# An FFN for two batches as seven block products, with weight sums kept as int8 and widened by GpSimd

## The chip, the cores and the metric

The kernel runs on one core of one Trainium2 chip. The metric is the device time of one execution in microseconds (us); the median of three runs is given. A core has TensorE (PE, matrix products; its weight loads are listed as PEld), VectorE (DVE), ScalarE (ACT), GpSimd (POOL) and SyncE (SP, which here only issues DMAs). Each engine works through its own instructions in order and waits for the others by semaphores. SBUF is the on-chip memory that all of them read, PSUM the one that PE writes its sums to.

## The reference

A cross-attention layer and a feed-forward layer (FFN), 16 batches of 128 rows, width 1024, float32:

```python
x = x + xattn(layernorm(x), ctx, ctx, Wq, bq, Wk, bk, Wv, bv, Wo, bo)   # 32 query heads, 8 key heads of 32
x = x + ffn(layernorm(x), kernel, scale)

def ffn(x, kernel, scale):                 # kernel: 1024 x 1024 booleans, one in ten is true
    x_ei = concat([x[..., :819], -4.0 * x[..., 819:]], axis=-1)
    return scale * einsum('bsi,if->bsf', x_ei, kernel.astype(float32))
```

So the FFN's weights are 0, 1 or, in the last 205 rows, -4 and 0 once the factor is moved into them. Their block sums and differences are small integers.

## The kernel before

Batches go in eight groups of two (`GB = 2`). For a group the kernel projects keys, values and queries, does attention in four units (a batch and half of the heads each), projects the output (`out_proj`) and does the FFN. Stages of three groups run at the same time: while the attention of group g runs, PE is given the output projection of group g-1, the key, value and query projections of group g+1, and then the FFN of a finished group.

The order of all engines' instructions is written out by hand. `Stream` holds a queue of generators and a list of timed events. A generator (`prep_v`, `ffn`, ...) issues a few matmuls and yields the microseconds that the author gives them; `Stream.run` takes pieces from the queue, adds these to `stream.now`, and fires every event that is due (`later(us, fn)`). `attend` starts an attention unit and sets the events for its maxima, exponentials, division and transposes. What stands in an event or a generator is thus issued at a planned time; at run time each engine keeps that order and waits for what isn't there.

- Query and output projections are done by `seven`: a 2x2 block product in seven products instead of eight (Winograd's form, L462). Left or right sums `s1..s4`, `t1..t4` come from DVE (L507, L644) or, for weights, from DRAM where they were stored once (`combine`, L782). Two PSUM buffers (`ps_mm`, `bufs=2`) hold the running sums `u` and `c`, then `v`; after each product `read` lets DVE add the buffer into the result (L676 for the output projection), and PE may go on in that buffer only when DVE has read it.
- The FFN (`ffn`, L738) is done batch by batch: two column halves x 8 chunks of 128 rows x 2 parts = 32 matmuls of 128x128 by 128x512 at L323. The activations are split in two float32r parts, `x2h` (rounded, ACT, L729) and `x2l` (the rest, DVE, L732), whose products add to the full accuracy; the weights, exact in float32r, lie in SBUF as `wf_sb`, converted once from bytes by ACT (`convert_ffn`, L258). DVE scales and adds each half into the residual `x` (L751), and SP writes it out (L759).
- Normalizing a row (`normalize`, L285) takes DVE for statistics, one small POOL operation for the root (`rs_a` for the input, `rs_f` for the FFN, L291) and DVE again (L292). The normalized rows of all but the last group go through DRAM and come back as 32x32 blocks in a `turn` tile (`through_dram`, L302), which DVE transposes. The last group's are transposed by PE (`ffn_transpose`).
- `get_x` (L887) loads the input rows of a later group (`xn`, in a `turn` tile too) and sets `rows_x`, statistics and normalization, 5 and 9 us behind. `load_residual` (L172) loads `x` a second time, for the residual, into one of three `x` tiles, and POOL adds the output bias (L180) in four pieces.

In the loop over groups the order at the end of a group is `qs[nxt]`, `get_x`, `prep_ctx`, then the FFN of both batches; the FFN of the last three groups comes in the last group's attention and behind it.

Of the kernel before, what the change touches and what calls it, by code (L numbers as in the profile page):

```python
# [10 lines left out]
FR = mybir.dt.float32r  # L11
U8 = mybir.dt.uint8
AF = mybir.ActivationFunctionType
ALU = mybir.AluOpType
# [8 lines left out]
class Stream:  # L23
# [28 lines left out]
    def run(self, until, keep=lambda: False):  # L52

        while self.now < until or keep():
            while self.events and min(self.events)[0] <= self.now:
                self.fire()
            if not self.piece():
                if not self.events:
                    return
                self.fire()  # L60

    def drain(self):
        while self.queue or self.events:
            self.run(self.now + 1.0)


def mixed(dense, light, skip=0, every=1):


    for n, us in enumerate(dense):  # L70
        yield us
        if n >= skip and (n - skip) % every == 0:
            yield next(light, 0.0)
    yield from light

# [7 lines left out]
def kernel(  # L83
# [47 lines left out]
    wv_sb = const.tile([P, NC, KV], FP, name="wv_sb")  # L131
    wf_sb = const.tile([P, NC, F], FR, name="wf_sb")
    bqT = const.tile([P, NA, NG], FP, name="bqT")
# [4 lines left out]

    xs, xns, cs = {}, {}, {}


# [24 lines left out]
    def load_x(b, tag="row"):  # L166

        x_t = work.tile([P, D], FP, tag=tag, name=f"xn{b}", bufs=2)
        nc.sync.dma_start(out=x_t, in_=x[b])
        xns[b] = x_t  # L170

    def load_residual(b, us=4.0, tag="x"):  # L172
# [37 lines left out]


    PIECE = 1024
    RING = 8
# [44 lines left out]
    def convert_ffn():  # L258

        row_w = const.tile([P, 1], FP, name="row_w")  # L260
        nc.gpsimd.memset(row_w, 1.0)
        nc.gpsimd.affine_select(
            out=row_w,
            in_=row_w,
            compare_op=ALU.is_ge,
            fill=w_inh,
            base=n_exc % P - 1,
            pattern=[[0, 1]],
            channel_multiplier=-1,
        )  # L270
        def chunk_(c):
            raw = raws[c // (NC // 2)][:, c % (NC // 2)]
            if (c + 1) * P <= n_exc:
                nc.scalar.copy(wf_sb[:, c], raw)
            else:
                w = w_inh if c * P >= n_exc else row_w
                nc.scalar.activation(wf_sb[:, c], raw, AF.Copy, scale=w)

        for c in range(NC):
            stream.later(2.0 * c, lambda c=c: chunk_(c))  # L280

# [20 lines left out]
    def through_dram(row, name, store, back, turn, then):  # L302

        there = dram.tile([P, D], FP, name=f"dram_{name}")

        def load():
            c_t = work.tile([P, NB, NC, 32], FP, tag="turn", name=f"turn_{name}", bufs=2)
            src = there.rearrange("(t r) (k n) -> k r t n", r=32, k=NB)
            for k in range(NB):
                dst = c_t[k * 32 : (k + 1) * 32].rearrange("r t c f -> r t (c f)")  # L310
                nc.sync.dma_start(out=dst, in_=src[k])
            stream.later(turn - back, lambda: then(c_t))

        stream.later(store, lambda: nc.sync.dma_start(out=there, in_=row) and None)
        stream.later(back, load)

# [10 lines left out]
    cTs, xTs, kTs, vs, qTs = {}, {}, {}, {}, {}  # L327
    HC = NC // 2

    def turned(store, srcs, grp, h, name, batches=range(GB)):  # L330
# [3 lines left out]
        for j in batches:  # L334
            b = grp * GB + j
            src = srcs.pop(b) if h == 1 else srcs[b]
            tp = ps_tp.tile([P, HC, P], FP, tag="tp", name=f"tp_{name}{b}_{h}")
            for c in range(HC):
                at = (h * HC + c) * P
                nc.tensor.transpose(tp[:, c], src[:, at : at + P], ident)  # L340
            nc.scalar.copy(store[grp, h][:, :, j * S : (j + 1) * S], tp)
            yield 0.45

# [12 lines left out]
    def rows_x(b):  # L356
# [5 lines left out]
        row = work.tile([P, D], FP, tag="row", name=f"xq{b}", bufs=2)  # L362
        normalize(by_quadrant(row), by_chunk(src), stats, f"a{b}")
        through_dram(row, f"x{b}", 2.5, 7.0, 7.0, lambda c_t: rows.update({b: c_t}))

    def turn_x(b, h):
        grp, j = b // GB, b % GB
        if (grp, h) not in xTs:
# [4 lines left out]
            c_t[:, :, h * HC : (h + 1) * HC],  # L373
        )

    def prep_ctx(grp, *us):
# [85 lines left out]
    def seven(name, product_of, read):  # L462
# [18 lines left out]
        read(u, "c21")  # L481

    PRODUCTS = ["a11 b11", "a12 b21", "s2 t2", "s1 t1", "s3 t3", "s4 b22", "a22 t4"]

# [135 lines left out]

    x2Ts, x2ns, x2stats = {}, {}, {}

    def out_proj(grp):
# [12 lines left out]
        def run():  # L636
# [36 lines left out]
            def read(mm, c):  # L673
# [7 lines left out]
                if c in ("c12", "c21"):  # L681
                    def norm():
                        b = b0 + j
                        x2n = work.tile([P, D], FP, tag="row", name=f"x2n{b}", bufs=2)
                        if b < B - GB:
                            normalize(by_quadrant(x2n), by_chunk(x_t), stats[j], f"f{b}")
                            through_dram(x2n, f"f{b}", 3.0, *FBACK[j], lambda t: split_blocks(b, t))
                        else:
# [10 lines left out]

    def new_parts(b):  # L700
        hi = work.tile([P, NC, S], FR, tag="x2h", name=f"x2h{b}", bufs=2)
        lo = work.tile([P, NC, S], FR, tag="x2l", name=f"x2l{b}", bufs=2)
        x2Ts[b] = (lo, hi)

    def ffn_transpose(b):

        new_parts(b)
        lo, hi = x2Ts[b]
        src = x2ns.pop(b)
        for h in range(NC // 4):  # L710
            tp = ps_tp.tile([P, 4, P], FP, tag="tp", name=f"tp_f{b}_{h}")
            for j in range(4):
                c = 4 * h + j
                nc.tensor.transpose(tp[:, j], src[:, c * P : (c + 1) * P], ident)
            cut = slice(4 * h, 4 * h + 4)
            nc.scalar.copy(hi[:, cut], tp)
            nc.vector.tensor_tensor(lo[:, cut], tp, hi[:, cut], ALU.subtract)
            yield 0.45

    def split_blocks(b, c_t, h=0):  # L720

        if h == 0:
            new_parts(b)
        lo, hi = (
            part[:, HC * h : HC * (h + 1)].rearrange("p c (t n) -> p t c n", t=NB) for part in x2Ts[b]
        )
        blocks = c_t[:, :, HC * h : HC * (h + 1)]
        nc.vector.transpose(blocks, blocks)
        nc.scalar.copy(hi, blocks)  # L729

        def rest():
            nc.vector.tensor_tensor(lo, blocks, hi, ALU.subtract)  # L732
            if h == 0:
                split_blocks(b, c_t, 1)

        stream.later(2.0, rest)

    def ffn(b):  # L738
        parts, x_t = x2Ts.pop(b), xs.pop(b)
        for h in range(F // HALF):  # L740
            cut = slice(h * HALF, (h + 1) * HALF)
            mm = ps_mm.tile([P, HALF], FP, tag="mm", name=f"f_{b}_{h}")
            pairs = [(part[:, c], wf_sb[:, c, cut]) for c in range(NC) for part in parts]
            for us in accumulate(mm, pairs):
                yield us / 4

            parts_ = 2 if b == B - 1 and h == F // HALF - 1 else 1
            for k in range(parts_):
                n = HALF // parts_
                at, some = slice(h * HALF + k * n, h * HALF + (k + 1) * n), slice(k * n, (k + 1) * n)  # L750
                nc.vector.scalar_tensor_tensor(  # L751
                    x_t[:, at], mm[:, some], fscale, x_t[:, at], ALU.mult, ALU.add
                )
                if b == B - 1:
                    queue = nc.scalar if k else nc.sync
                    queue.dma_start(out=out[b][:, at], in_=x_t[:, at])
            yield 0.43
        if b < B - 1:
            nc.sync.dma_start(out=out[b], in_=x_t)  # L759

    def attend(b, a, length):
# [18 lines left out]
        return pts  # L780

    def combine(w, k, part, engine=nc.gpsimd):  # L782

# [9 lines left out]
        for dst, left, right, op in ops:  # L793
            for h in range(2):
                cols = slice(h * HALF, (h + 1) * HALF)
                engine.tensor_tensor(dst[:, cols], left[:, cols], right[:, cols], op)  # L796
            yield
        for n, t in enumerate(order):
            nc.sync.dma_start(out=sums[w, n + 1, k], in_=t)

# [15 lines left out]
    def load_o_part(k):  # L816

        part = {}
        for r in range(2):
            for o in range(2):  # L820
                tag = ("x2h", "x2l")[o]
                t = work.tile([P, PIECE], FP, tag=tag, name=f"wo{k}_{r}_{o}", bufs=2)
                nc.sync.dma_start(out=t.rearrange("p (c n) -> p c n", c=2), in_=o_block(r, o, k))
                part[r, o] = t
        return part
# [4 lines left out]
    with tc.manual_schedule():  # L830
# [67 lines left out]
        def get_ctx(grp):  # L898
            if grp < NGRP:
                for j in range(GB):  # L900
                    load_ctx(grp * GB + j)

        def residuals(grp):
            for j in range(GB):
# [22 lines left out]
        for grp in range(NGRP):  # L927
# [18 lines left out]
            elif more:  # L946
# [8 lines left out]
                    qs[nxt],  # L955
                    once(get_x, nxt + 1),
                    once(prep_ctx, nxt + 1, 2.5, 7.0, 11.0, 16.0),
                )

                if nxt < NGRP - 1:  # L960
                    stream.add(ffn(p0), once(load_residual, b1, 2.0), ffn(p1))
            else:
# [3 lines left out]
                    once(load_residual, b0, 4.0, "ctx"),  # L966
                    ffn(p0 - 2),
                    once(load_residual, b1, 4.0),
                    ffn(p1 - 2),
                )  # L970
# [21 lines left out]
            os[NGRP - 1],  # L992
            ffn(B - 4),
            mixed(ffn(B - 3), ffn_transpose(B - 2), 10, 2),
            mixed(ffn(B - 2), ffn_transpose(B - 1), 8, 2),
            ffn(B - 1),
        )
# [50 lines left out]
```

## Time and profile before

The runs took 788.64, 786.96 and 786.23 us. The profiled execution has a span of 783.8 us.

| What | us |
|---|---|
| median of the runs | 786.96 |
| span of the profiled execution | 783.8 |
| PE busy in 700.0 to 724.0 (the last group's attention, with an FFN) | 23.4 of 24.0 |
| PE busy in 748.7 to 783.8 (the last two groups' FFN, output) | 31.2 of 35.1 |
| DVE busy in these two | 15.1 and 12.6 |
| POOL busy in these two | 5.4 and 0.8 |
| FFN matmuls, L323 `f` | 512 |
| POOL operations in the whole span | 142, 114.6 us |

A line of the group view reads: source line, engine, operation, what is written from what, shape, count, then busy time and mean duration, then the engine's idle time just before these and what ended it. A chain line reads: start, duration, engine, tile and line, count. Matmul durations in the profile overlap each other, since PE is pipelined; the spacing of a run of equal matmuls tells what one costs.

### The profile page before, as it was taken

What the parts mean: (1) busy time and instruction counts of PE and PEld (TensorE: products, weight loads), DVE (VectorE), ACT (ScalarE), POOL (GpSimd) and SP (SyncE); (2) the same over time, 40 slices, a digit from 0 to 9 for tenths busy, and PEclk for the clock granted to TensorE, in tenths of its full rate; (3) what the DMA queues carried; (4) which work ended last, traced back from release to release, by engine and by line L of the source; (5) the groups of instructions that cost most, each with busy time, mean ns of one, the idle gap of its engine ahead of it and who ended that gap; (6) DMA issues with size and microseconds to landing.
All of it is one profiled execution on the core that took longest, in us unless ns stands there. A gap on an engine that the chain in (4) does not pass through costs nothing.

```text
span 783.8 us, 13740 instructions
## 1 busy us (share of the span) xinstructions
PE 765.3 (98%) x5008; PEld 570.7 (73%) x5008; DVE 488.7 (62%) x887; ACT 323.1 (41%) x1261; POOL 114.6 (15%) x142
## 2 busy tenths in 40 slices
PE   5999999999999999999999999999999999999997
PEld 4877884689747986479855898558985689456476
DVE  1358648756766667466784667755676666765552
ACT  0244854435234453344433444344434445575100
POOL 4066502010100102020020200202001010103000
PEclk9999999999999999999999999999999999999999
DMA  9999899969698777878688795977769667763702
GB/s 241 317 332 316 327 342 372 271 196 304 236 299 237 235 237 233 293 215 262 222 270 264 192 290 207 307 230 206 265 216 313 207 199 235 253 202 103 264 27 81
DMA packets 99412, 192.42 MB, mean 245 GB/s; under 512 B 8256, under 2 KB 57728, under 8 KB 99344
## 3 DMA queue, kind: packets, MB, share of 16 engines
q1 hardware_dynamic: 97568, 189.30, 75.4%
q10 hardware_dynamic: 1248, 1.11, 0.6%
q0 software_dynamic: 528, 1.12, 0.6%
q8 instruction: 40, 0.66, 0.4%
q14 instruction: 28, 0.23, 0.1%
HBM read 161.09 MB, written 30.41 MB: 244 GB/s over the span
## 4 chain that ended last, share of the span: by engine, by line
PE 87%; DMA 6%; DVE 4%; POOL 1%; issue 1%; SPq 0%; ACT 0%; DVEq 0%; POOLq 0%
PE f L323 14%; PE o_u L662 13%; PE q_u L451 13%; PE o_v L662 7%; PE tpp L601 7%; PE q_v L451 7%; PE v L323 6%; PE k L323 5%; PE sc L568 4%; PE av L611 4%; PE q_c L451 3%; PE o_c L662 3%; DMA ctx<-in_ctx_dram 2%; DMA wo<-in_L_xattn_Wo_dram 1%; DMA piece<-in_L_xattn_Wq_dram 1%; POOL wo L796 1%
## 5 line engine op out<-in xcount | busy, mean ns | idle before, releaser
L584 ACT ACTIVATE p<-sc,negm 128x128 f32<-128x128 f32 x512 | 181.4, 369 | 133.2 <-DVE negm L580 73.1
L603 ACT COPY pt<-tpp 128x512 f32<-128x512 f32 x128 | 74.7, 591 | 146.8 <-PE tpp L601 146.5
L580 DVE TENSOR_REDUCE negm<-sc 128x4 f32<-128x512 f32 x128 | 86.8, 680 | 45.6 <-PE sc L568 45.6
L584 ACT ACTIVATION_READ_ACCUMULATOR p<-sc,negm 128x1 f32 x512 | 105.5, 206 | 0.0
L323 PE MATMUL f<-wf_sb,x2l 128*128 128x512 f32 x256 | 104.3, 407 | 0.0
L323 PE MATMUL f<-wf_sb,x2h 128*128 128x512 f32 x256 | 100.5, 393 | 0.0
L596 DVE TENSOR_TENSOR p<-p,inv 128x512 f32<-128x512 f32 x128 | 91.9, 718 | 4.4
L451 PE MATMUL q_u<-t,piece 128*128 128x128 f32 x672 | 81.3, 275 | 0.0
L601 PEld LDWEIGHTS tpp<-ident,p 128*128 128x128 f32 x512 | 61.9, 141 | 24.6 <-issue 16.7
L601 PE MATMUL tpp<-ident,p 128*128 128x128 f32 x512 | 75.9, 273 | 3.4 <-DVE p L596 3.2
L451 PEld LDWEIGHTS q_u<-t,piece 128*128 128x128 f32 x672 | 78.1, 192 | 0.1
L180 POOL TENSOR_TENSOR x<-x,bo_b 128x256 f32<-128x256 f32 x64 | 54.3, 874 | 154.7 <-DMA x<-in_x_dram 154.7
L323 PE MATMUL v<-wv_sb,cT 128*128 128x256 f32 x256 | 61.2, 388 | 9.5 <-DMA wv_sb<-in_L_xattn_Wv_dram 7.7
L662 PE MATMUL o_v<-piece,s 128*128 128x512 f32 x128 | 60.3, 598 | 0.5 <-DVE x L676 0.5
L662 PE MATMUL o_u<-piece,s 128*128 128x512 f32 x128 | 59.2, 594 | 0.6 <-DVE x L676 0.6
L323 PEld LDWEIGHTS v<-wv_sb,cT 128*128 128x128 f32 x256 | 47.8, 194 | 16.2 <-DVE cT L349 9.2
L662 PE MATMUL o_u<-piece,yT 128*128 128x512 f32 x128 | 58.6, 600 | 0.0
L323 PE MATMUL k<-cT,wk_sb 128*128 128x256 f32 x256 | 58.0, 380 | 0.0
L323 PEld LDWEIGHTS f<-wf_sb,x2l 128*128 128x128 f32 x256 | 48.2, 188 | 10.5 <-issue 1.1
L323 PEld LDWEIGHTS f<-wf_sb,x2h 128*128 128x128 f32 x256 | 48.2, 188 | 9.6 <-issue 0.5
L323 PEld LDWEIGHTS k<-cT,wk_sb 128*128 128x128 f32 x256 | 47.9, 190 | 8.8 <-issue 2.6
L568 PEld LDWEIGHTS sc<-kT,qT 32*128 32x128 f32 x1024 | 31.4, 186 | 25.7 <-issue 25.7
(86 smaller groups left out, 938.1 us busy)
## 6 DMA issues: line engine op xcount, KB each, us to landing
piece<-o SPq DMA_DIRECT2D x64, 512.0 KB, 4.6
piece<-q SPq DMA_DIRECT2D x56, 512.0 KB, 5.1
piece<-in_L_xattn_Wq_dram SPq DMA_DIRECT2D x50, 512.0 KB, 5.0
piece<-in_L_xattn_Wo_dram SPq DMA_DIRECT2D x48, 512.0 KB, 4.7
xn<-in_x_dram SPq DMA_DIRECT2D x16, 512.0 KB, 6.8
x<-in_x_dram SPq DMA_DIRECT2D x16, 512.0 KB, 5.1
ctx<-in_ctx_dram SPq DMA_DIRECT2D x60, 128.0 KB, 6.7
out_dram<-x SPq DMA_DIRECT2D x15, 512.0 KB, 2.7
```

The costliest lines, as they stand in the source:

```text
L180: lambda cut=cut: nc.gpsimd.tensor_add(x_t[:, cut], x_t[:, cut], bo_b[:, cut]) and None,
L323: nc.tensor.matmul(mm, lhsT=lhsT, rhs=rhs, start=k == 0, stop=k == n - 1)
L451: nc.tensor.matmul(mm if part is None else mm[:, part], lhsT=lhsT, rhs=rhs, start=start and n == k == 0, stop=k == len(some) - 1, skip_gro ...
L568: nc.tensor.matmul(tiles[i][:, g], lhsT=qT[rows, g], rhs=kT[rows, a, cols], start=True, stop=True,)
L580: nc.vector.tensor_reduce(negm, tile_, AX.X, ALU.max, negate=True)
L584: nc.scalar.activation(p[:, g], tile_[:, g], AF.Exp, bias=negm[:, g : g + 1], accum_out=total[:, g : g + 1],)
L596: nc.vector.tensor_mul(p, p, inv.unsqueeze(2).to_broadcast([P, NG, S]))
L601: nc.tensor.transpose(tp[:, g], p[:, g], ident)
L603: nc.scalar.copy(pt, tp)
L611: nc.tensor.matmul(mm[i * HD : (i + 1) * HD], lhsT=vs[b][:, h * HD : (h + 1) * HD], rhs=pts[i], start=True, stop=True,)
L662: nc.tensor.matmul(mm, lhsT=lhsT[:, 2 * k + c], rhs=w[:, c], start=start and k == c == 0, stop=k == c == 1, skip_group_check=True,)
L796: engine.tensor_tensor(dst[:, cols], left[:, cols], right[:, cols], op)
```

## The change

The FFN takes two batches at once, as a 2x2 block product (batch by half of the inputs, half of the inputs by half of the outputs) in seven products. A product has 4 chunks x 2 parts, so a group takes 56 matmuls where two batches took 64.

The weights' blocks and sums (`b11 b21 b22 t1 t2 t3 t4`) are made once, by ACT and DVE, and lie in SBUF as int8 (seven blocks of four chunks, 14 KiB a partition where 32 were used). `widen` copies the next chunk to a float32r tile on POOL; there are eight such tiles (`WIDE`), and each chunk that PE has used calls for the next. The activations' sums `s1..s4` are made by POOL, in the `turn` tiles themselves for all but the last group, and each of the seven left blocks is split in its two parts when it is due (`split`, at most four in being). So `turn` tiles are held until the last block is split; `turning` counts their users, and `when` holds back a load until one is free. For that reason `get_x` is moved behind the FFN. The pieces of `Wo` that are summed at the start are loaded and stored as halves, in the tiles of the two parts.

```diff
+    wf_sb = const.tile([P, 7, NC // 2, F // 2], I8, name="wf_sb")
...
+    FFN = {"b11": 0, "b21": 1, "b22": 2, "t1": 3, "t2": 4, "t3": 5, "t4": 6}
+    WIDE = 8
+    wide = []
+    WANTED = [(prod.split()[1], c) for prod in PRODUCTS for c in range(NC // 2)] * (B // GB)
+    def widen():
+        if WANTED:
+            name, c = WANTED.pop(0)
+            t = work.tile([P, HALF], FR, tag="wide", name=f"wide{len(WANTED)}", bufs=WIDE)
+            nc.gpsimd.tensor_copy(t, wf_sb[:, FFN[name], c])
+            wide.append(t)
...
-        stream.later(back, load)
+        stream.later(back, lambda: stream.when(lambda: len(turning) < 2, load))
...
+    def split_now(grp, name):
+        hi = work.tile([P, HC, S], FR, tag="x2h", name=f"x2h{grp}_{name}", bufs=4)
+        lo = work.tile([P, HC, S], FR, tag="x2l", name=f"x2l{grp}_{name}", bufs=4)
+        blocks = halves[grp][name]
+        nc.scalar.copy(hi.rearrange(BLOCK, t=NB), blocks)
+        def rest():
+            nc.vector.tensor_tensor(
+                lo.rearrange(BLOCK, t=NB), blocks, hi.rearrange(BLOCK, t=NB), ALU.subtract
+            )
...
+        stream.later(1.3, rest)
+    def sum_blocks(grp):
...
+            nc.gpsimd.tensor_tensor(half[dst], half[left], half[right], op)
+        for n, name in enumerate(("s2", "s1", "s3", "s4", "a22")):
+            stream.later(4.5 + 1.5 * n, lambda name=name: split(grp, name))
...
+    def ffn(grp, done_with=lambda j: None):
...
+            for c in range(HC):
+                w = wide.pop(0)
+                for n, part in enumerate(both):
+                    nc.tensor.matmul(
+                        mm,
+                        lhsT=part[:, c],
+                        rhs=w,
+                        start=start and c == n == 0,
+                        stop=c == HC - 1 and n == 1,
+                        skip_group_check=True,
+                    )
+                widen()
+                yield 0.46
...
+        yield from seven(f"f{grp}", product_of, read)
...
                     qs[nxt],
-                    once(get_x, nxt + 1),
                     once(prep_ctx, nxt + 1, 2.5, 7.0, 11.0, 16.0),
                 )
                 if nxt < NGRP - 1:
-                    stream.add(ffn(p0), once(load_residual, b1, 2.0), ffn(p1))
+                    stream.add(ffn(grp - 1, residual(b1, 2.0)))
+                stream.add(once(get_x, nxt + 1))
...
             os[NGRP - 1],
-            ffn(B - 4),
-            mixed(ffn(B - 3), ffn_transpose(B - 2), 10, 2),
-            mixed(ffn(B - 2), ffn_transpose(B - 1), 8, 2),
-            ffn(B - 1),
+            inserted(ffn(NGRP - 2), {5: ffn_transpose(B - 2), 16: ffn_transpose(B - 1)}),
+            ffn(NGRP - 1),
```

After each product `read` lets DVE scale and add the PSUM buffer into `x` (seven reads a group). When the first batch is complete, behind the sixth product, SP writes it out and `done_with` calls `load_residual`; when the second is, behind the seventh, it is written out too.

## The prediction

> **What bounds the kernel now.** First the busy line of the page.
>
> ```profile
> PE 765.3 (98%) x5008; PEld 570.7 (73%) x5008; DVE 488.7 (62%) x887; ACT 323.1 (41%) x1261; POOL 114.6 (15%) x142
> ```
>
> Then the windows view of one inner feed-forward stretch: start and end, length, and busy time of PE, PEld, DVE, ACT and POOL, then the granted clock and the DMA share.
>
> ```profile
> 195.30:212.10 16.80, 16.80 (x87) 13.62 (x89) 12.42 (x25) 4.91 (x19) 1.10 (x2) 1.00 0.63 217
> ```
>
> Then the chain of work that ended last, in order of time.
>
> ```profile
> 207.92 4.14 PE f L323 x18
> 214.16 3.63 PE o_u L662 x8
> 217.79 3.43 PE o_c L662 x8
> 221.22 3.43 PE o_u L662 x8
> ...
> 748.73 12.38 PE f L323 x54
> ```
>
> PE (TensorE) is the bound: busy 98%, at a granted clock of 1.00 in that window, and the chain runs through it almost without a gap. Line L323 `f` is the feed-forward network (FFN): 12.38 us / 54 = 0.229 us a matmul (the group view's 0.40 us overlaps its neighbours, so the chain's spacing is the price). The inner stretch runs on the chain from 195.57 to 207.92 + 4.14 = 212.06 us: 64 x 0.229 = 14.66 us, plus four attention transposes at 0.46 = 16.49 us. POOL (GpSimd) is nearly idle, DVE (VectorE) is not: 12.4 of 16.8 us.
>
> Then the group view by shapes (busy us, mean ns), for what POOL can do.
>
> ```profile
> masks.py:199 POOL TENSOR_SCALAR_AFFINE_SELECT ident<-ident 128x128 f32<-128x128 f32 x1 | 0.3, 306 | 0.1
> ...
> L262 POOL TENSOR_SCALAR_AFFINE_SELECT row_w<-row_w 128x1 f32<-128x1 f32 x1 | 0.2, 187 | 0.1
> ```
>
> One input, one output: 187 ns plus (306 - 187)/127 = 0.94 ns an element. And the timeline (start, duration) of POOL beside DVE:
>
> ```profile
> 44.56 8.31 POOL L796 TENSOR_TENSOR wo<-wo,wo 128x512 f32<-128x512 f32 x6 [0.22 <-DMA wo<-in_L_xattn_Wo_dram]
> 47.91 0.92 DVE L596 TENSOR_TENSOR p<-p,inv 128x512 f32<-128x512 f32 x1
> 52.34 1.08 DVE L596 TENSOR_TENSOR p<-p,inv 128x512 f32<-128x512 f32 x1
> ...
> 78.84 3.73 POOL L796 TENSOR_TENSOR wo<-wo,wo 128x512 f32<-128x512 f32 x3
> ```
>
> Two inputs of 512: 3.73/3 = 1.24 us where DVE ran no operation with two SBUF inputs; six took 8.31 instead of 7.46 while DVE ran three such (`p<-p,inv`). Each overlap so cost POOL 0.28 us, and DVE 0.2 to 0.4 us over the 0.69 us that the same `p` takes elsewhere.
>
> Last the timelines of DVE and of SP's queue (SPq) around the end of the stretch.
>
> ```profile
> 196.01 0.86 SPq L169 DMA_DIRECT2D xn<-in_x_dram  x2
> 201.97 1.29 DVE L283 BATCH_NORM_STATS2 st_a<-xn 128x6 f32<-128x512 f32 x2 [0.89 <-DMA xn<-in_x_dram]
> 204.42 0.81 DVE L292 TENSOR_SCALAR xq<-xn,mv_a,rs_a 128x1024 f32<-128x1024 f32 x1 [0.73 <-POOL rs_a L291]
> 206.55 0.34 SPq L759 DMA_DIRECT2D out_dram<-x  x1
> 209.30 0.33 SPq L174 DMA_DIRECT2D x<-in_x_dram  x1
> 217.83 0.69 DVE L676 TENSOR_TENSOR x<-o_u,x 128x512 f32<-128x512 f32 x1 [0.40 <-PE o_u L662]
> ```
>
> An `xn` load lands 5.9 us after issue; a residual load waits 2.75 us on SP until the output that holds its buffer is written; and DVE reads the first product of the output projection at once, 5.8 us after the stretch's end.
>
> **Matmuls removed.** Two batches took 64 FFN matmuls and take 7 products x 4 chunks x 2 parts = 56. Eight fewer x 0.229 = 1.84 us a group, 14.7 us in eight groups, all on the path. That is the whole gain.
>
> **Widening added.** Each 128x512 chunk of weights is copied from int8 to float32r by POOL just before its two matmuls: 28 a group, ring of 8. PE uses one in 0.458 us. No int8 copy is in the trace. From above: the add with two inputs, 1.24 us. From below: PE's own 0.458 us, under which the copy costs nothing. I take the row that it is nearest to, the select: 0.187 + 511 x 0.94 ns = 0.67 us. In the built order DVE has eight operations with two SBUF inputs inside the stretch (three `p`, five subtractions for the lower parts): 8 x 0.28 = 2.2 us, 0.10 a widening, so 0.77 us. Eight chunks are in stock; the 28th needs the 20th widening: 0.56 (first chunk used, and the signal) + 20 x 0.77 = 15.96, and with its own 0.46 + 0.1 the stretch takes 16.5 us, against 14.65 if only PE counted. So the 1.84 us is given back: zero for the five inner stretches. Bounds: -9.2 us in all (POOL keeps up) to 5 x (0.56 + 20 x 1.24 + 2.2 + 0.56 - 16.5) = +58 us.
>
> [...]
>
> **Splitting and reading added.** A group gets 7 casts on ACT (were 4), 7 subtractions (were 4) and 7 scaled reads (were 4) on DVE: 3 x 0.62 on ACT, 3 x 0.69 + 3 x 0.74 = 4.3 us on DVE. DVE's stretch becomes about 12 us at its spacing of 0.61 a row, plus 8 x 0.3: 14.5 of 16.5 us. Hidden, by the POOL pace; were POOL fast, DVE would be the next cover to go, at up to 1 us a stretch. The four block sums on POOL, 4 x 1.24 = 5 us a group, stand in the quiet part ahead of the stretch and wait for DMAs already due.
>
> **The loads that move.** `get_x` now follows the FFN, and its normalization is placed 5 us behind that end. What it is moved past: on SP the output of the first batch, the residual load and the second output. Let t be the end of the last matmul. The sixth product is read by about t - 2.2 (the last product at POOL's pace, 4 x 0.77 = 3.1, less 0.1 + 0.75); its output goes out, the residual load waits 2.75 (t + 0.5), `xn` issues at t + 1.3 and lands at t + 7.2. In the built DVE order `st_a` stands before the second score maximum and **before the read of the first output-projection product**. So DVE waits, then 1.29 (statistics), 0.4, 0.7 (POOL's `rs_a`), 0.75 (`xq`), 0.6 (maximum), 0.69 (read): t + 11.7. PE wants that accumulator at t + 9.2 (two products of 3.43 behind the scores). Stall 2.5 us. The second batch's chain stands before the second read: two `p`, a maximum, two reciprocals, statistics, `rs_a`, `xq`, 5.3 us, then 0.69; PE has a product of 3.43 meanwhile. Stall 2.5 us again. Queued behind both are the score maxima and with them ACT's exponentials. Five groups: +25 us. Bounds: 0 (landing early, all absorbed) to 6.3 x 5 = 31 (last product at PE's pace, so everything 1.3 us later). I take 25: it follows from rows.
>
> **The last group's own FFN.** Before, `rs_f` on POOL is a link of the chain there twice (709.75 and 716.85 us). Now widenings stand ahead of each: about one and a half of them, 1 us each time: +2, from -2 (PE's eight matmuls won) to +8 (ten widenings ahead of the first).
>
> **The end.** Before: 128 x 0.229 + 1.8 of transposes = 31.1 us from 748.73, then 3.9 to the end. After, PE alone: 112 x 0.229 + 1.8 = 27.4, a gain of 3.8. POOL: 48 widenings x 0.67 = 32.2, four block sums 5.0, one `rs_f` 0.55, twelve overlaps with DVE 3.4: 41.1; with 0.56 ahead and 0.56 behind, 42.2, so +11. Bounds -3.8 and +39 (1.24 a widening).
>
> **The start.** Sixteen int8 subtractions on DVE (11 us at 0.69) and eight first widenings (5.4 us), while DMA and PE have other work: +1, 0 to +4. The Wo loads cut in halves move the same bytes: nothing.
>
> Sum: 0 + 25 + 2 + 11 + 1 = +39 on the profiled span of 783.8. The median of the runs, 786.96, lies 3.2 above that span: **826 us**.
>
> **Rivals.**
> *PE's gain stays.* If the copy takes 0.46 us or less and `xn` is in time, the sum is -14.7 + 1: about 773 us. For it: PE at 98%, POOL at 15%. Against it: the select row, and the order on SP and DVE. It decides against my side when a widening including overlaps stays under 0.68 us ((14.65 - 0.46 - 0.56)/20) and the wait of `st_a` under 3 us. Chance 0.18.
> *One half only.* POOL paces, but the moved loads hurt nobody: 0 + 0 + 2 + 11 + 1, 801 us; or POOL is fast and the loads alone stall, -14.7 + 31 + 1, 804 us. Chance 0.18 together.
> *POOL at the price of two inputs.* 58 + 25 + 8 + 39 + 4 = +134: some 920 us. [...] Against it: a copy reads half of what an add reads. Chance 0.06.
> *They cancel.* POOL fast and stalls near 15 us: 787 us, chance 0.03. That the matmuls would not fall is out: the built order holds 448.
> My forecast, both mechanisms: 0.55, own range 806 to 850.
>
> **How the numbers follow.** Times within 0.3% (2.4 us) are what a measurement of this kernel can't tell from no change. Faster 0.18, same 0.03, slower 0.55 + 0.18 + 0.06 = 0.79. The range goes down to 771, to take in most of the faster case, and up to 862, a widening of about 0.85 us; outside lie the price of two inputs and the lowest faster times.
>
> **What would show it.** The widening's mean: above 0.6 us confirms the pace, under 0.5 refutes it. The wait list: PE `f` behind POOL `wide` in the inner stretches (about 1.8 us each) and at the end (15 us); DVE `st_a` behind DMA `xn`, 3 to 5 us, five times; PE `o_u` and `o_v` behind DVE `x` reads, 2.5 us each. `f` matmuls: 448 at 0.229 us spacing where not waiting. If the inner stretches come out near 14.7 us and the PE gaps after them below 1 us, I am wrong, and the time is under 785.

## The result and the profile after

The changed kernel takes 860.87 us (median of 4 runs, 860.11 to 862.05), against 787.17 us before (4 runs): 1.0933 times, 95% interval 1.0917 to 1.095. The profiled execution spans 858.9 us against 783.8, 75.1 us more; the forecast was 39. The page's busy line, and the granted clock in its 40 slices:

```profile
PE 782.8 (91%) x4944; PEld 566.1 (66%) x4944; DVE 550.6 (64%) x951; ACT 336.5 (39%) x1291; POOL 311.8 (36%) x398
...
PEclk9999997999999999999989999899998999999979
```

PE has 64 matmuls fewer, as planned, yet it is busy for 782.8 us instead of 765.3: in the kernel before, its granted clock is 1.00 from 8 to 783 us; now it is lower at its stalls (0.50 and then 0.61 at the early one of 9.51 us), and eight matmuls of the output projection behind that one take 6.01 us, where eight ahead of it took 3.70. The waits come on top. The chain of work in order of time gives four marks at the same product of each kernel, `q_u` in the last quarter of a group. Before (start, duration):

```profile
103.37 3.57 PE q_u L451 x32
...
191.99 3.57 PE q_u L451 x32
...
567.19 3.57 PE q_u L451 x32
...
653.83 3.57 PE q_u L451 x32
```

After:

```profile
104.78 3.57 PE q_u L508 x32
...
205.51 3.59 PE q_u L508 x32
...
612.99 3.59 PE q_u L508 x32
...
708.06 3.57 PE q_u L508 x32
```

The differences of such marks, for all kernels run, tell where each one loses (us of the profiled execution; "one inner group" is the time from the second to the third mark, divided by four; the mark near 104 itself moves between 103.0 and 105.9 from run to run). Each row but its last number is one execution, and the four runs of a kernel lie 1.6 to 6.7 us apart, so small differences between the last rows say nothing:

| kernel | first to second mark | one inner group | third to fourth | fourth to end | median of the runs |
|---|---|---|---|---|---|
| before | 88.62 | 93.80 | 86.64 | 129.97 | 787.17 |
| after | 100.73 | 101.87 | 95.07 | 150.84 | 860.87 |
| weight sums later | 90.47 | 101.85 | 95.09 | 150.90 | 849.91 |
| normalization later | 100.31 | 94.85 | 87.63 | 150.25 | 821.50 |
| no widening | 100.31 | 100.64 | 95.12 | 132.94 | 837.20 |
| tail: half the widenings on ACT | 100.31 | 101.89 | 95.39 | 144.94 | 853.16 |
| tail: block sums on DVE too | 100.31 | 102.04 | 95.28 | 142.34 | 852.10 |
| tail: transposes later, nothing else | 100.32 | 102.09 | 95.42 | 147.52 | 857.76 |
| normalization later, half on ACT | 99.66 | 94.40 | 87.23 | 141.69 | 812.12 |
| four edits together | 90.86 | 94.78 | 87.63 | 140.78 | 805.07 |
| these, half on ACT throughout | 90.48 | 94.54 | 87.25 | 140.01 | 803.41 |
| and transposes later | 90.00 | 94.38 | 87.23 | 141.13 | 802.41 |
| and context transposes later | 94.92 | 94.65 | 87.52 | 138.74 | 802.59 |
| and sixth group's sums on GpSimd | 92.86 | 94.65 | 87.52 | 137.54 | 804.33 |

So the change loses 12 us early, 8.1 us in each of five groups (4 x 8.07 + 8.43 = 40.7), and 21 us in the last group and the end.

**Early.** The timeline of the changed kernel, DVE's rows, then PE's (in brackets the idle time ahead, and what ended it):

```profile
113.82 0.69 DVE L315 TENSOR_TENSOR wf_sb<-wf_sb 128x512 int8<-128x512 int8 x1
...
117.46 15.41 DVE L315 TENSOR_TENSOR wf_sb<-wf_sb 128x512 int8<-128x512 int8 x15
132.79 0.68 DVE L635 TENSOR_REDUCE negm<-sc 128x4 f32<-128x512 f32 x1
...
135.97 0.68 DVE L731 TENSOR_TENSOR x<-o_u,x 128x512 f32<-128x512 f32 x1
...
136.70 6.01 PE L717 MATMUL o_u<-piece,s 128*128 128x512 f32 x8 [9.51 <-DVE x L731]
```

Fifteen sums of weights stand in one row, 15.4 us, ahead of a score maximum and of the read of the first output-projection product. PE needs that read's accumulator and stands idle for 9.5 us. (The planner had spaced the sums 3 us apart, but its list of dense work ran empty there, and then all that is due later is issued at once.) The 16 sums average 1.073 us; the first one, alone, took 0.69.

**Behind an inner stretch.** The timeline of the group at 209 us, SP's queue, DVE and PE:

```profile
225.57 0.34 SPq L875 DMA_DIRECT2D out_dram<-x  x1
...
228.24 0.33 SPq L185 DMA_DIRECT2D x<-in_x_dram  x1
...
229.14 1.82 SPq L178 DMA_DIRECT2D xn<-in_x_dram  x2
...
235.27 1.29 DVE L335 BATCH_NORM_STATS2 st_a<-xn 128x6 f32<-128x512 f32 x2 [4.58 <-DMA xn<-in_x_dram]
...
239.38 0.68 DVE L731 TENSOR_TENSOR x<-o_u,x 128x512 f32<-128x512 f32 x1
...
240.11 5.40 PE L717 MATMUL o_u<-piece,s 128*128 128x512 f32 x8 [4.39 <-DVE x L731]
...
245.29 0.68 DVE L731 TENSOR_TENSOR x<-o_c,x 128x512 f32<-128x512 f32 x1
```

The row is the one that the prediction described: the residual load waits 2.67 us for an output, `xn` issues behind it, the statistics wait for it, and behind them stand the reads. PE idles 4.39 us ahead of the second use of `o_u`, and its next product starts at 246.03 where it could have at 243.5: 6.9 us. (In the second of these stalls PE itself is idle for only 0.53 us, because the product before it takes 5.40 us, at a granted clock of 0.57 from 240 to 244 us, where the first one ahead of the stalls took 3.70; the read at 245.29 would have held PE until 246 in any case.)

**Inside an inner stretch.** The windows view of it (columns as in the prediction). On the chain the stretch runs from 209.10 to 226.56 us, 17.5 us against 16.49 before:

```profile
208.97:226.58 17.61, 15.36 (x78) 11.72 (x80) 14.69 (x22) 7.23 (x23) 16.97 (x24) 1.00 0.20 64
```

GpSimd (POOL) is busy for 16.97 of 17.61 us, as predicted. But PE doesn't wait for it. The timeline of the two engines has the 20th widening, and the first matmul of the 28th chunk, which needs it:

```profile
223.89 0.61 POOL L331 CAST wide<-wf_sb 128x512 fp32r<-128x512 int8 x1
...
225.94 0.39 PE L846 MATMUL f_u<-wide,x2l_a 128*128 128x512 f32 x1
```

The widening was done 1.4 us before PE used it, and each of the 19 ahead of it 1.5 to 3.4 us. The waits view puts two waits of PE's weight loads, 1.6 and 1.5 us, down to GpSimd; but the widenings needed there had been done for 2.5 and 3.4 us. PE's own two waits in the stretch, 1.18 and 1.08 us, were ended by reads on DVE. The timeline of the second shows why these come late:

```profile
217.19 0.90 DVE L651 TENSOR_TENSOR p<-p,inv 128x512 f32<-128x512 f32 x1
218.01 1.09 DVE L775 TENSOR_TENSOR x2l_s<-turn_f,x2h_s 128x512 fp32r<-128x512 f32 x1
219.02 0.74 DVE L868 SCALAR_TENSOR_TENSOR x<-f_u,fscale,x 128x512 f32<-128x512 f32 x1
219.91 0.47 PE L846 MATMUL f_u<-wide,x2l_s 128*128 128x512 f32 x1 [1.08 <-DVE x L868]
```

The operations ahead of the read, 0.69 us each before, take 0.90 and 1.09 us beside the widenings.

### The profile page after: what moved, and what is told of

It is laid out like the page before. It is cut to its first block, busy times and chain, and to the rows that moved or that the text cites. A ratio compares the mean times of both kernels' runs of the same rounds, so it can differ in the third digit from the quotient of the medians.

```text
span 858.9 us, 14201 instructions
## 1 busy us (share of the span) xinstructions
PE 782.8 (91%) x4944; PEld 566.1 (66%) x4944; DVE 550.6 (64%) x951; ACT 336.5 (39%) x1291; POOL 311.8 (36%) x398
## 4 chain that ended last, share of the span: by engine, by line
PE 69%; DVE 17%; DMA 7%; POOL 5%; issue 1%; ACT 1%; SPq 0%; DVEq 0%; ACTq 0%; POOLq 0%
PE q_u L508 12%; PE o_u L717 9%; PE o_v L717 6%; PE q_v L508 6%; PE k L376 6%; PE v L376 6%; PE tpp L656 5%; PE f_u L846 4%; DMA xn<-in_x_dram 3%; PE sc L623 3%; PE av L666 3%; PE q_c L508 3%; DVE p L651 3%; POOL wide L331 2%; DVE x2l_s L775 2%; PE q L376 2%
## 5 line engine op out<-in xcount | busy, mean ns | idle before, releaser
L331 POOL CAST wide<-wf_sb 128x512 fp32r<-128x512 int8 x224 | 155.9, 742 | 46.5 <-PE f_u L846 44.0
L717 PE MATMUL o_u<-piece,s 128*128 128x512 f32 x128 | 73.4, 714 | 31.4 <-DVE x L731 31.4
L651 DVE TENSOR_TENSOR p<-p,inv 128x512 f32<-128x512 f32 x128 | 95.8, 748 | 4.4
L717 PEld LDWEIGHTS o_u<-piece,s 128*128 128x128 f32 x128 | 27.8, 231 | 67.4 <-DVE x L731 38.1
L376 PE MATMUL v<-wv_sb,cT 128*128 128x256 f32 x256 | 63.3, 397 | 9.5 <-DMA wv_sb<-in_L_xattn_Wv_dram 7.8
L801 POOL TENSOR_TENSOR s<-turn_f,turn_f 128x512 f32<-128x512 f32 x8 | 10.7, 1335 | 148.3 <-DMA piece<-in_L_xattn_Wo_dram 65.2
L343 POOL TENSOR_TENSOR rs_f<-ve_f,minus_half 128x1 f32<-128x1 f32 x16 | 8.8, 547 | 153.5 <-DVE ve_f L341 99.5
L376 PEld LDWEIGHTS v<-wv_sb,cT 128*128 128x128 f32 x256 | 48.9, 199 | 17.1 <-DVE cT L403 9.4
```

Of the source, the lines that this page charges most:

```text
L331: nc.gpsimd.tensor_copy(t, wf_sb[:, FFN[name], c])
L376: nc.tensor.matmul(mm, lhsT=lhsT, rhs=rhs, start=k == 0, stop=k == n - 1)
L651: nc.vector.tensor_mul(p, p, inv.unsqueeze(2).to_broadcast([P, NG, S]))
L717: nc.tensor.matmul(mm, lhsT=lhsT[:, 2 * k + c], rhs=w[:, c], start=start and k == c == 0, stop=k == c == 1, skip_group_check=True,)
```

## The experiments

**Weight sums later.** The sums go out from the start of the next group:

```diff
+    def sum_weights():
...
-                2.0 * n + 8.0 + 3.0 * m,
+                8.0 + 3.0 * m,
...
+                    *([once(sum_weights)] if grp == 1 else []),
```

> The sixteen int8 weight sums stay on VectorE but are issued from the start of the next group, 3 us apart on the planner's clock, where they stood in one row between the query read and the next unit's score maximum. Theory (the row of sums held back the read that the first output projection needs and so delayed the second group's query products by 13.5 us): the query products of the second group start about 167 to 169 us instead of 179.8, no row of sums longer than 1.1 us, total 861 - 12 = about 849 us (845 to 852). Rival (the first group is late for the conversions on ScalarE or the moved loads, and the sums only lie there): no change, 859 to 862 us. Second rival (VectorE is so full that sixteen sums cost the same wherever they are): the second group grows by 10 us and the total stays at 858 to 862 us.

Measured: 849.91 us (1.0803 times before, 1.0785 to 1.0822). The chain of that kernel:

```profile
105.04 3.57 PE q_u L510 x32
...
195.51 3.59 PE q_u L510 x32
```

90.5 us between these marks instead of 100.7: 10.3 of the 12.1 us come back. The row of sums is the cause, and both rivals of the expectation fall. The slice of 0.7 at that place in the PEclk line is gone too.

**Normalization later.**

```
-    stream.later((10.0 if grp == 2 else 5.0) + 4.0 * j, lambda b=b: rows_x(b))
+    stream.later((10.0 if grp == 2 else 14.0) + 4.0 * j, lambda b=b: rows_x(b))
```

> The loads of x stay behind the FFN; only the normalization that waits for them comes later: 14 and 18 us behind the load on the planner's clock instead of 5 and 9. In VectorE's order the statistics then stand behind the reads of the first two output-projection products. Theory (VectorE waits 4.6 us for the load and holds those reads; PE loses 4.4 + 2.5 = 6.9 us in each of five groups): total 861 - 34 = about 827 us (822 to 833), PE's wait for the reads of the output projection falls from 31 us to under 8. Rival (the place of the stall only moves: the query rows come back too late for the next group's products): 840 to 860 us, with PE q_u behind DVE xT. Second rival (the stretch and not the stall makes a group 8 us longer): no change.

Measured: 821.50 us (1.0442, 1.0425 to 1.0458), 39 us less. Its timeline behind the same stretch:

```profile
227.20 1.78 SPq L178 DMA_DIRECT2D xn<-in_x_dram  x2
...
230.38 0.69 DVE L731 TENSOR_TENSOR x<-o_u,x 128x512 f32<-128x512 f32 x1 [1.03 <-PE o_u L717]
```

DVE now waits for PE there, and no longer the other way round. A group takes 94.85 us instead of 101.87, and 35.5 of the 40.7 us of the five groups are back: 7.1 us a group. The loads stand where the change put them and go out just as late; only the place of what waits for them in DVE's order was wrong. The 1.05 us a group that are left against before are the longer stretch (1.0 us).

**No widening.**

```
-                widen()
+                wide.append(w)
```

> Left out: every widening after the first eight; the FFN's later chunks multiply with these eight widened tiles again. All else stays. Theory (GpSimd paces only the tail; in the inner stretches the reads on VectorE do): inner stretches 16.5 to 17.5 us instead of 17.6, the stalls behind them stay at about 6.9 us a group, the last group 2 to 3 us shorter, the tail 10 to 13 us shorter: total 861 - 5 x 0.8 - 2.5 - 12 = about 843 us (838 to 848). Rival, as predicted (GpSimd paces the inner stretches too): these fall to 14.7 us, total 830 to 835 us. Second rival (the widening hinders VectorE throughout, through whatever they share): below 828 us.

Measured: 837.20 us (1.0644, 1.0626 to 1.0662). It ended just below the 838 to 848 that the theory gave, and above the 830 to 835 of the rival. The group view (busy us, mean ns, idle time ahead) shows what the widening did to DVE. In the changed kernel:

```profile
L331 POOL CAST wide<-wf_sb 128x512 fp32r<-128x512 int8 x224 | 155.9, 742 | 46.5 <-PE f_u L846 44.0 <-PE f_c L846 1.9 <-PE f_v L846 0.6
...
L775 DVE TENSOR_TENSOR x2l_s<-turn_f,x2h_s 128x512 fp32r<-128x512 f32 x21 | 21.9, 1047 | 1.2 <-ACT x2h_s L772 1.2
```

Without widening:

```profile
L775 DVE TENSOR_TENSOR x2l_s<-turn_f,x2h_s 128x512 fp32r<-128x512 f32 x21 | 15.7, 753 | 1.2 <-ACT x2h_s L772 1.2
```

The same subtraction takes 0.753 us instead of 1.047. On the chain the stretch runs from 208.16 to 224.09, 15.9 us. That is 1.5 us less than with widening; since no widening came late there, it is what the widenings cost DVE. The stretch is still 1.3 us longer than PE alone would need (14.65 in the prediction): the row of softmax, splits and reads on DVE and ACT. Of the 1.5 us the group keeps 1.2. The last group and the end, 132.94 us, get back 17.9 of their 20.9 extra us: that loss belongs to the widening.

**Tail: half the widenings on ScalarE (ACT).**

```
+            if len(WANTED) < 56 and len(WANTED) % 2 == 0:
+                nc.scalar.copy(t, wf_sb[:, FFN[name], c])
```

> Of the last 56 widenings (the last two groups' FFN) every other one goes to ScalarE. Theory (in the tail GpSimd paces PE: 48 widenings, eight sums and one power are 40 of its 53 us): the tail of 76.7 us falls to 64 to 68, total about 850 us (847 to 853). Rival (the tail waits for the chain sums, split, product, read, and GpSimd's widenings lie beside it): at most 3 us less, 858 to 861 us.

Measured: 853.16 us (1.084, 1.0822 to 1.0858): 7.7 us less, the fourth column 5.9 less. That is just above the theory's 847 to 853 and well below the rival's 858 to 861; the tail fell from 76.7 to 71.4 us, where 64 to 68 was expected. So GpSimd's rate costs about a third of the 17.9 us that the widening costs there. The timeline of the changed kernel shows this part:

```profile
830.35 23.91 POOL L331 CAST wide<-wf_sb 128x512 fp32r<-128x512 int8 x37
```

These widenings follow each other without a gap, 0.65 us each, where PE needs 0.458 us a chunk, and from 837.5 us on each of the last 27 chunks starts 0.05 to 0.07 us behind the end of its widening: 27 x 0.19 = some 5 us. Here GpSimd does set the pace. The chain shows the other part:

```profile
803.01 0.69 DVE x L731
...
807.20 1.29 POOL turn_f L801
808.49 0.52 POOL rs_f L343
...
810.85 2.05 PE f_c L846 x4
...
824.08 3.00 POOL s L801 x2
...
830.40 1.03 POOL wide L331
831.47 1.22 PE f_u L846 x2
```

GpSimd is asked for three things in one order: block sums (`turn_f`, `s`, L801), the power `rs_f`, and widenings. From 803 to 810.9 and from 823.4 to 831.5 us the chain runs by these and the operations on DVE behind them; PE has gaps of 2.6, 3.6 and 3.8 us that end at 810.9, 818.8 and 831.5. While PE waits for sums or the power, the ring of eight is full and GpSimd can't widen ahead.

**Tail: block sums on DVE too.** `engine = nc.vector if grp >= NGRP - 2 else nc.gpsimd` for the sums, with the edit above.

> The alternate widening of the last 56 as before (it alone gave 853.2 us), and the block sums of the last two groups on VectorE instead of GpSimd. Theory (PE's idle time of 8 us before the second-half products of the sixth FFN, and about 4 us ahead of the first power of the normalization, are GpSimd's eight block sums of 1.3 to 1.7 us that stand ahead of a widening and of the power): the tail falls by 9 to 12 us, total about 843 us (840 to 846). Rival (the row of normalization, transposition, copy and split sets the tail whoever sums): at most 4 us less, 849 to 853 us.

Measured: 852.10 us (1.0828, 1.0809 to 1.0846). The theory falls, and the rival's 849 to 853 holds: 1 us, not 9 to 12, and the intervals overlap. The idle time ahead of `f_u` shrinks, but the windows view shows what PE does then (length, busy times, granted clock third from the end):

```profile
821.00:826.00 5.00, 2.78 (x13) 1.94 (x11) 4.91 (x7) 4.32 (x8) 2.12 (x3) 1.00 0.00 0
826.00:829.00 3.00, 2.79 (x9) 2.23 (x10) 3.00 (x5) 0.74 (x2) 1.23 (x2) 0.76 0.02 5
829.00:832.00 3.00, 3.00 (x11) 2.40 (x9) 1.15 (x3) 1.85 (x4) 1.23 (x2) 0.67 0.00 0
```

Sums of 1 us each keep DVE busy for 4.91 of 5 us there, the split still comes at the end of the row, and behind a gap of 2.4 us PE runs at 0.67 to 0.76 of its clock.

**Tail: transposes later, nothing else.** `{5: ..., 16: ...}` in the sixth FFN becomes `{14: ..., 22: ...}`.

> Only the place of the last two batches' transposes changes: behind the 14th and the 22nd step of the sixth FFN in the planner's count instead of the 5th and the 16th, that is behind about 16 and 32 of its 56 matmuls instead of 12 and 20. If GpSimd's rate sets the tail (the prediction: 48 widenings, sums and overlaps are 42 us of work), nothing is to be had by order: 859 to 862 us. If PE's waits for the normalized rows in that place set it (8 us ahead of the first and 4 us ahead of the second pair in the earlier runs), the total falls by 4 to 8 us: 853 to 857 us.

Measured: 857.76 us (1.0895, 1.0874 to 1.0916), 3.1 us less, between the two: order has a share, a small one.

**Half the widenings on ACT everywhere**, with the normalization later.

> The later normalization as before (it alone gave 821.5 us), and every other widening of the whole kernel on ScalarE. Theory (in the inner stretches GpSimd's widenings stretch VectorE's operations with two SBUF inputs from 0.69 to 0.8-1.09 us, and VectorE's row of them with the reads paces PE): x2l_s mean falls from 1.05 to about 0.85 us, the inner stretch from 17.5 to about 16.6 us, and with the tail's 7.7 us (the alternate run's gain) the total is 821.5 - 7.7 - 5 x 0.9 = about 809 us (806 to 812). Rival (ScalarE has no room in the stretch: 14 x 0.62 = 8.7 us beside 5 us of exponentials, and its delay holds the attention transposes on PE): stretch 17.5 us or longer, total 814 to 830 us.

Measured: 812.12 us (1.0341, 1.0306 to 1.0376): 9.4 us less, 12.5 expected. Its groups:

```profile
L334 POOL CAST wide<-wf_sb 128x512 fp32r<-128x512 int8 x112 | 77.1, 694 | 93.9 <-PE f_u L849 71.2 <-PE f_v L849 17.2 <-PE f_c L849 4.8
L332 ACT CAST wide<-wf_sb 128x512 fp32r<-128x512 int8 x112 | 68.3, 630 | 30.9 <-PE f_u L849 19.5 <-PE f_v L849 7.5 <-PE f_c L849 3.8
...
L778 DVE TENSOR_TENSOR x2l_s<-turn_f,x2h_s 128x512 fp32r<-128x512 f32 x21 | 17.7, 847 | 1.2 <-ACT x2h_s L775 1.2
```

The subtraction falls to 0.847 us, as expected, and a group by 0.45 us, half of what was expected. This is the test of the pace: with 14 widenings a group, GpSimd has half the work, and the stretch still takes 17.1 us (206.39 to 223.46), 0.4 less. So the rate of GpSimd doesn't set the stretch; the reads on DVE, which PE waits for, do (a chain further down shows their row).

**Together.** Weight sums later (from 28 us, 2 us apart), normalization later, and in the tail half on ACT and sums on DVE.

> Together: weight sums in the next group (now from 28 us on, 2 us apart), normalization later, in the tail every other widening on ScalarE, block sums of the last two groups on VectorE. If the four losses are separate, as the theory has it, they add: 860.9 - 11 - 2.5 (the weight sums now behind the busy stretch) - 39.4 - 7.7 - 10 = about 790 us (786 to 795); what is left against before would be the inner stretches (+1.0 a group) and the last group (+3). If two of them are the same wait seen twice, 798 us or more.

Measured: 805.07 us (1.0238, 1.02 to 1.0276). The expectation had counted 10 us for the sums on DVE, whose own run gave 1. With the measured gains, 860.9 - 11.0 - 39.4 - 8.8 = 801.7 us: they add but for some 3 us.

**And half on ACT throughout.**

> As the run of all four together, but every other widening of the whole kernel on ScalarE. Theory: 5 x 0.9 us less than that run, and 1 to 2 us in the last group: about 784 us (779 to 788), so at or a little below the time before. Rival (ScalarE has no room): 3 us or more above the run of all four.

Measured: 803.41 us (1.0206, 1.0181 to 1.023): not told apart from the run above, and not at the time before.

**And transposes later; and the context transposes later; and the sixth group's sums back on GpSimd.** Three kernels, each with one edit more, the third with two: `{14, 22}`; `once(prep_ctx, nxt + 1, 20.0, 22.0, 24.0, 26.0)` for `2.5, 7.0, 11.0, 16.0`; sums on DVE only for the last group with `{18, 26}`.

> The run with all four edits and half the widenings on ScalarE (803.4 us), and the transposes at the later place. Theory (there GpSimd has room, so what is left of the tail's loss, 10 us against before, is PE idle in front of the transposes, and the slower clock behind each idle stretch): 6 to 8 us less, 795 to 798 us. Rival (the row of block sums and splits behind the last transposes only ends later by as much): no change, 802 to 805 us.

> As that run, and the four transposes of the next context group on VectorE, three of which stand in the inner FFN stretch, come 17.5 to 10 us later, behind the stretch. Theory (VectorE's row paces the stretch; 3 x 0.6 us leave it): the inner stretch falls from about 16.7 to 15.5 us, the group by 1 to 1.5 us, total 5 to 8 us below that run: 788 to 792 us. Rival (they stand in the way of the output projection's reads or come too late for the key products instead): the same as that run or up to 10 us more.

> As the run with the later context transposes, but the sixth group's block sums back on GpSimd (the seventh's stay on VectorE), and the transposes of the last two batches at steps 18 and 26. Theory (at the end of the last output projection VectorE has the reads, statistics and four sums in a row; GpSimd has nothing): the tail falls by another 2 to 3 us, 785 to 789 us. Rival (GpSimd's 1.3 us a sum and the power behind them are the longer way): 1 to 3 us more than that run.

Measured: 802.41 us (1.0196, 1.0178 to 1.0214), 802.59 (1.0198, 1.0172 to 1.0224) and 804.33 (1.021, 1.0177 to 1.0243). All three theories fall, and their rivals, which expected no change or a few us more, hold; nothing moved outside the intervals. The second tells most. With three transposes fewer on DVE the stretch (201.95 to 219.22) takes 17.3 us, no less than the 17.1 of the kernel before it, and its chain says why:

```profile
203.55 1.09 DVE x2l_s L780
...
205.42 0.94 DVE p L656
...
207.26 0.77 ACT p L644 x4
...
209.04 0.69 DVE x2l_s L780
209.86 0.90 DVE p L656
210.75 1.01 DVE x2l_s L780
211.77 0.67 DVE x L874
...
212.57 0.70 PE f_u L852 x2
```

What was taken out wasn't in the row that ends last: that row is split, read, softmax, split, read, alternately on DVE and ACT, and its long members, 0.90 to 1.09 us, are those with two SBUF inputs (the read of a PSUM buffer, `x`, has 0.67 there). The first 10.6 us of the stretch go by it. In the column from the first to the second mark the second and third kernels lose 4.9 and 2.9 us more than the first. The second differs from the first only by the later context transposes; but the first's profile is the fastest of its four runs and the second's the slowest, so how much of this is scatter is open.

No version beat the kernel before. The best is some 2% slower; of its 15.7 us (spans 799.5 and 783.8) the marks put 11.2 in the last group and the end, 2.9 in the five groups and 1.6 ahead of them.

## Why the prediction was right, and where not

The direction was right, and the moved loads acted as described. GpSimd's pace, the second mechanism, held at the end but not in the inner stretches, and the size was far off: 39 us forecast, 75 on the span, 73.7 between the medians, with every term too small. The time lies outside the 806 to 850 that the prediction gave to its own case. That the whole range holds it, 1.1 us below its top, is luck: the top of 862 stood for a slower widening, of about 0.85 us, and the widenings took 0.742. (Nor does that top follow: with 100 widenings on the path in the inner stretches and 48 at the end, 0.85 us instead of 0.67 adds 27 us, to 853.) By its terms:

- **Start, +1: measured +12.1.** This is the worst step: the sums' 11 us were costed from rows, and then hidden "while DMA and PE have other work". The cover was named without looking at the order on DVE: the sums stand in one row ahead of reads that PE waits for. The fifteen in the row also took 15.4 us, because a sum took 1.07 us on average and not 0.69; 11 had been counted for all sixteen.
- **Loads that move, +25: measured 35.5** (what the later normalization gave back in the five groups; 6.9 us a group in the trace). The mechanism is shown: the same loads with their statistics placed later cost nothing. The size is 4.5 us above the stated upper bound of 31. The sum had taken the last product at GpSimd's pace (3.1 us), so that the output went out early; it ran at PE's, the output left 1.0 us before the end of the stretch instead of 2.2, and `xn` landed at t + 8.7, not t + 7.2. Both stalls were there: 4.4 and 2.5 us, against 2.5 and 2.5.
- **Inner stretches, 0: measured +1.0 each.** The widening's mean, 0.742 us, is close to the 0.77 of the sum and well above the 0.6 that was to confirm the pace; GpSimd was 96% busy, and the waits view even has the weight loads behind `wide`. None of these signs could tell. The step "the 28th needs the 20th widening" isn't what decides: the 20th was done 1.4 us early, and with half of GpSimd's work gone the stretch lost only 0.4 us. The term that failed is "DVE 14.5 of 16.5 us, hidden, by the POOL pace". The 14.5 was right (14.69), the hiding was not: PE waits on the reads at the end of that row. The matmul gain is lost through GpSimd's hindrance of DVE (1.5 us, the run without widening) and the row itself (1.3 us). The aside that DVE is next at up to 1 us a stretch is about that 1.3. Two busy engines told nothing of which one paced; the releaser of PE's waits did.
- **Last group's own FFN, +2: measured +3.4** (from the fourth mark to the first product of the last output projection 74.1 us, 70.7 before, 71.4 in the run without widening). `rs_f` stands behind widenings, as said.
- **The end, +11: measured +17.4** (59.3 to 76.7 us). Its cause is mostly the widening: in the run without it the end takes 61.5 us. But the sum added GpSimd's busy times as though it worked without a gap. It was busy for 40.4 of the last 53 us, because the ring keeps it from running ahead while PE waits for sums and powers; only behind these does it set the pace. Half on ACT, then sums on DVE too, and another order alone brought back 5.9, 8.5 and 3.3 us of the last column's 20.9. What holds the last 8 to 11 us of the best versions is not settled.

As to the rivals: the moved loads and the widening are both real, so "one half only" is out, though its price for a fast GpSimd (-14.7) would not have come either: without widening the stretch was 15.9, not 14.65. Of the 0.28 us that the sum had for an overlap with DVE: in the inner stretch an operation on DVE lost up to 0.40 us (1.09 against 0.69), and a widening took up to 1.08 us, where an undisturbed one took 0.61.

## What to carry to other kernels

When work is put on an idle engine, cost it twice: its own time, and what it does to the operations of the engine beside it (here 0.742 us a widening, and on DVE a subtraction of 1.047 us that took 0.753 without); and "hidden" needs the row of operations that the hidden work stands in, and the first reader behind it. The loads that were made later cost little by themselves; what stood behind their first consumer in DVE's order cost 7.1 us a group, and moving that consumer cured it (39 us for one number). An engine's busy share (here GpSimd's 16.97 of 17.61 us) didn't tell what paced the stretch: take away half of its work and look, or compare when each result was ready with when it was used.

## What the runs showed of the hardware

The granted clock was lower at PE's stalls of 9.51 and 4.39 us (0.57 from 240 to 244 us at the second). The windows view of the changed kernel around the early stall (granted clock third from the end):

```profile
132.00:136.00 4.00, 0.00 (x0) 0.00 (x0) 3.97 (x6) 1.50 (x8) 2.91 (x4) 0.50 0.09 34
136.00:143.00 7.00, 6.30 (x10) 2.76 (x11) 6.90 (x15) 4.03 (x22) 0.00 (x0) 0.61 0.22 63
```

It is 0.50 in the stall's last 4 us and 0.61 in the 7 us behind it, 1.00 after that. Eight matmuls behind the stall took 6.01 us, where the two products of eight ahead of it took 3.70 and 3.60. In the run with the tail's sums on DVE, a gap of 2.4 us at 823.8 came ahead of clocks of 0.76 and 0.67: from 827.7 to 830.7 us the matmuls start 0.43 us apart instead of 0.23. Not every gap shows it: behind the one of 2.20 us that ends at 61.39 us in the changed kernel, the clock was 1.00 (59 to 75 us). With the stalls behind the stretches gone, in the run with the later normalization, the three slices marked 8 in the middle of the PEclk line were marked 9.

Widening a 128x512 block from int8 to float32r took 0.61 us on GpSimd where nothing disturbed it (a row of four, from 226.69 us on, took 2.29 us) and 0.63 on ACT (the mean of 112 in the run with half on ACT): undisturbed, GpSimd was no slower than ACT for this copy. Its cost was elsewhere: on DVE, beside it, the subtraction took 1.05 us instead of 0.75.
